# Softmax sums, folds and statistics placed differently in a planned attention kernel: all sums on VectorE, and a planner that keeps GpSimd and VectorE's two-operand sums apart

## The chip, the cores and the metric

The kernel runs on one core of a Trainium2 chip. The metric is the device time of one execution in microseconds (us), and the median over several executions counts. The engines of the core run side by side, each through its own queue of instructions in order: TensorE (PE in the profile, with PEld for its weight loads), VectorE (DVE), ScalarE (ACT), GpSimd (POOL) and SyncE (SP), which here issues nearly all DMAs. They meet through semaphores.

## The reference

A cross attention is followed by a small recurrent state space layer, all in float32:

```
xn   = layernorm(x)          # x: 4096 x 512
cn   = layernorm(ctx)        # ctx: 3202 x 512
x    = x + softmax(q(xn) k(cn)^T / 8) v(cn) W_o + b_o      # 8 heads of 64
U    = (layernorm(x) W_in + b_in) B                        # 4096 x 64
s_t  = silu(s_{t-1} A^T) + u_t                             # over the 4096 rows
out  = x + s C + mean(program_probs) W_prog + b_prog
```

## The kernel before

**Tiles and stages.** A first stage (to about 200 us) normalizes the context and writes keys and values to DRAM (`kd`, `vd`). Then comes the attention. The queries are cut into 8 blocks Q of 512 rows, the heads into 4 pairs `hp`, and each pair works on two halves of 256 queries. One such (Q, hp, half) is a *unit*; there are 64. A unit goes over the 3202 keys in `NDC` = 13 steps c of 256 keys (the last step is half as wide; two left-over keys are handled apart, as the "extra" tile). In each step:

- `scores` (PE, L635): eight matmuls on quarters of the array into one PSUM tile `s`. There are two such tiles (ring `s`).
- `weights` (ACT, L705): the exponential of the tile, PSUM to SBUF tile `p`, 128x1024. There are 18 such tiles (ring `p`).
- `product` (PE, L745): weights times values into the output accumulator `po` in PSUM. There is one such accumulator (ring `o`), so the first product of a unit waits until the last unit's has been emptied.
- `add` (L713): the weights are added elementwise into `acc`, 128x1024, to be the softmax's denominators. It is a tensor_tensor with both operands in SBUF. Step 1 adds the tiles of step 0 and 1, the others add to `acc`. Of the steps c = 2, 6 and 10 the add runs on GpSimd (`POOL_SUMS`), except in the last unit; all others run on VectorE.

After step 1, `rest` (VectorE, L699) adds the two left-over keys in two small instructions.

**The end of a unit** (`finish`): `output` (ACT, L780) copies one half of `po`, and `join` (VectorE, L784) adds the other half from PSUM, which frees `po`. `fold` (GpSimd, L720) adds the two halves of `acc`, `sums` (PE, L763, tile `pd`) adds over the partitions, two copies on ScalarE (L797) and `whole` (VectorE, L801) collect the denominators, `inverse` (VectorE, L804) takes the reciprocal, `scale` (VectorE, L811) multiplies the output by it, and `fall` (L807) sums it for a check.

**Beside the units.** For each block of queries: `queries` (layer norm, transposition and the query projection of the next block; `heads`, L312) and `project` (output projection `outs` L988, residual `x1` L1001, a second layer norm, the inputs `u` of the recurrence, L1044). Both use `norm_pieces`: `stats` (VectorE), `factors` (three small GpSimd instructions), `scaled` (ACT). GpSimd also adds two rows of constants, `row` (L982) and `mod` (L1005). Two halves of 128 rows belong together; each half's `stats` takes one of two places in the ring `fs`.

**The end of the kernel** (`drain`). The recurrence is computed by sweeps over 16 steps that repeat until start and end agree; sweep "a" runs beside the last units, sweep "b" and a chain for the last 256 rows (`last_rows`, L1420) after them. Each link of a chain goes PE (L1179), ACT (L1207, L1417), VectorE (L1214, L1420). `outputs` joins the states' products (L1253) with the rows (VectorE L1273; ACT L1267 and GpSimd L1270), and DMAs store them. Last comes a check: `differ` compares the sweeps, `nbad` (L1799) is read by all engines, and a branch skips a slow repair.

**What sets the order.** The order of all this is planned when the program is built. `Plan.add` records a piece: engine, an assumed cost in ns, the pieces that it follows, a due time, and the ring places that it takes and gives. `Plan.order` plays the pieces through: whenever an engine is free it takes, of those that are ready and find their ring places (`fits`), the one with the earliest due time. A piece on another engine can start `LATE` ns after the end of the one that it follows; `ENTER` and `LEAVE` are added where TensorE changes between quarter matmuls (`kind` "quarters") and full ones. Only the order comes of it. On the chip, each engine goes through its queue in that order and waits on semaphores. `from_(d)` ties a piece to the scores of the step at due time d, and `STEP` = 2150 ns is one step in due times.

Of the kernel before, what the change touches and what calls it, by code (L numbers as in the profile page):

```python
# [10 lines left out]
F32 = mybir.dt.float32  # L11
# [3 lines left out]
ALU = mybir.AluOpType  # L15
# [5 lines left out]
P = 128  # L21
# [4 lines left out]
NDC = NCH // 2  # L26
# [12 lines left out]
NP = 18  # L39
# [9 lines left out]
STEP = 2150  # L49
# [18 lines left out]
class Plan:  # L68
# [31 lines left out]
    def order(self):  # L100
# [10 lines left out]
        free = dict.fromkeys(self.LATE, 0)  # L111
        last, now, events, out = None, 0, [], []
# [58 lines left out]
def xattn_ssm_kernel(  # L171
# [534 lines left out]

    def add(w, c, engine):
# [5 lines left out]
        engine.tensor_tensor(  # L713
            w["acc"][:, :, :nb, :], t[:, :, :nb, :], before[:, :, :nb, :], ALU.add
        )

    def fold(w):

        acc = w["acc"]
        nc.gpsimd.tensor_tensor(acc[:, :, 0, :], acc[:, :, 0, :], acc[:, :, 1, :], ALU.add)  # L720

# [64 lines left out]
    def finish(w, i, d, plan):  # L786
# [22 lines left out]
        def scale(part):  # L809
# [28 lines left out]
    def norm_pieces(plan, ks, gets, d, after, names, gives, wait):  # L838
# [21 lines left out]
        for t, (k, v) in enumerate(zip(ks, vs)):  # L860
            plan.add((*k, "stats"), "DVE", 870, partial(stats_, v, gets[t], names[t]), [after[t]],
                     d + t, ["fs"])
            plan.add((*k, "factors"), "POOL", 2000, partial(factors_, v), [(*k, "stats")], d + 2000)
            plan.add((*k, "scaled"), "ACT", 800, partial(scaled_, v, gets[t], t),
                     [(*k, "factors")] + ([(*ks[0], "scaled")] if t else []) + wait, d + 3 * STEP + t,
                     [] if t else ["xh", "xh"], [("fs", (*k, "stats"))] + gives[t : t + 1])
        return vs
# [98 lines left out]
    def project(plan, Q, halves, d, index):  # L966

        for half in halves:
# [42 lines left out]
            for t in range(2):  # L1011
                plan.add((*ks[t], "load"), "SP", 800, partial(load, t),
                         [(*ks[0], "load")] if t else [from_(d - 6 * STEP)], d - 6 * STEP + t, [] if t else ["x"])
                plan.add((*ks[t], "row"), "POOL", 1300, partial(row, vs[t]), [(*ks[t], "load")], d - STEP)
            plan.add((*k2, "outs"), "PE", 7200, outs,
# [101 lines left out]
    AHEAD_K, AHEAD, REF = 10, 6, 5  # L1117
    POOL_SUMS = (2, 6, 10)
    A_PACE, B_PACE = 1500, 1900
# [359 lines left out]
    def unit(plan, i):  # L1479
# [30 lines left out]
        for c in range(NDC):  # L1510
# [17 lines left out]
            if c:  # L1528
                dve = w["last"] or c not in POOL_SUMS
                before = {1: ("weights", i, 0), 2: ("rest", i)}.get(c, ("add", i, c - 1))  # L1530
                plan.add(("add", i, c), "DVE" if dve else "POOL", (100 + 1200 * part) if dve else 2382,
                         partial(add, w, c, nc.vector if dve else nc.gpsimd),
                         [("weights", i, c), before], d + 1200,
                         ["acc"] if c == 1 else [],
                         [p] + ([("p", ("weights", i, 0))] if c == 1 else []))
            if c == 1:
                plan.add(("rest", i), "DVE", 1200, partial(rest, w), [("add", i, 1), ("extra", first)],
                         d + 1300, [], [("extra", ("extra", first))])
# [228 lines left out]
    with tc.manual_schedule():  # L1767
        for g in range(AHEAD_K):
            load_k(*steps[g])
        for g in range(AHEAD):  # L1770
            load_v(*steps[g])
        plan = Plan(
            dict(
                s=2, m=2, mt=1, o=1, p=NP, acc=3, extra=4, q=6, x=2, x1=1, xn2=1, fs=2,
                xn=1, xh=2, max=2, rd=2, o_=12,
# [113 lines left out]
```

## Time and profile before

| what | value |
|---|---|
| median of 3 runs | 2004.89 us (2004.11 to 2006.86) |
| the profiled execution's own time | 2004.45 us |
| its span | 2002.6 us |
| mean granted clock of TensorE | 0.995 |
| busy: PE, DVE, ACT, POOL | 1954.1, 1259.4, 1130.1, 789.5 us |
| scores (L635) and products (L745), 12800 matmuls each | 826.5 and 822.6 us |
| adds (L713) on VectorE, on GpSimd | 515 + 64, 189 |
| HBM | 93 GB/s over the span |

The profile shows one execution. "Busy" is time with an instruction of that engine in work; matmuls overlap and their ends are modelled, so a short wait of TensorE can be hidden behind the end of the matmul before, and the distance from one start to the next tells more. In a row of groups stand line, engine, operation, tiles and shapes, the number of instructions, busy us and mean ns of one, then the idle time of the engine in front of them and what ended it. In a row in order of time stand start, length, engine, line, operation, tiles, shapes, number, and in brackets the idle time in front.

### The profile page before, as it was taken

What the parts mean: (1) busy time and instruction counts of PE and PEld (TensorE: products, weight loads), DVE (VectorE), ACT (ScalarE), POOL (GpSimd) and SP (SyncE); (2) the same over time, 40 slices, a digit from 0 to 9 for tenths busy, and PEclk for the clock granted to TensorE, in tenths of its full rate; (3) what the DMA queues carried; (4) which work ended last, traced back from release to release, by engine and by line L of the source; (5) the groups of instructions that cost most, each with busy time, mean ns of one, the idle gap of its engine ahead of it and who ended that gap; (6) DMA issues with size and microseconds to landing.
All of it is one profiled execution on the core that took longest, in us unless ns stands there. A gap on an engine that the chain in (4) does not pass through costs nothing. (4 is left out here: it accounts for less than half of the span.)

```text
span 2002.6 us, 66617 instructions
## 1 busy us (share of the span) xinstructions
PE 1954.1 (98%) x29070; PEld 1251.4 (62%) x29070; DVE 1259.4 (63%) x1533; ACT 1130.1 (56%) x1478; POOL 789.5 (39%) x631
## 2 busy tenths in 40 slices
PE   8999999999999999999999999999999999999996
PEld 4444566666666666666666666666666666666764
DVE  4311367566866677667756785667766675667575
ACT  2233466566666566556656665666565666655552
POOL 2111234345533454245434543445334642444424
PEclk9999999999999999999999999999999999999998
DMA  5632323224332243123322332234322331444485
GB/s 173 192 100 66 101 80 97 58 79 111 106 79 79 82 112 92 59 81 90 107 65 79 106 107 73 79 95 113 86 78 59 101 92 52 148 142 144 129 207 182
DMA packets 246934, 204.28 MB, mean 102 GB/s; under 512 B 80808, under 2 KB 220072, under 8 KB 246636
## 3 DMA queue, kind: packets, MB, share of 16 engines
q1 hardware_dynamic: 242088, 192.28, 33.4%
q10 hardware_dynamic: 4548, 7.67, 1.2%
q8 instruction: 231, 3.78, 0.8%
q14 instruction: 67, 0.55, 0.1%
HBM read 156.32 MB, written 29.88 MB: 93 GB/s over the span
## 5 line engine op out<-in xcount | busy, mean ns | idle before, releaser
L705 ACT ACTIVATE p<-s,shifts 128x1024 f32<-128x1024 f32 (+1 forms) x832 | 883.2, 1080 | 559.7 <-PE s L635 540.0
L745 PE MATMUL po<-p,v 64*64 64x256 f32 x12800 | 822.6, 377 | 10.6 <-DVE o L784 10.6
L635 PE MATMUL s<-q,k 64*64 64x256 f32 x12800 | 826.5, 377 | 4.9 <-ACT p L705 3.9
L713 DVE TENSOR_TENSOR acc<-p,acc 128x1024 f32<-128x1024 f32 (+1 forms) x515 | 633.3, 1230 | 249.0 <-POOL acc L713 179.4
L713 POOL TENSOR_TENSOR acc<-p,acc 128x1024 f32<-128x1024 f32 x189 | 449.2, 2376 | 679.1 <-ACT p L705 362.2
L635 PEld LDWEIGHTS s<-q,k 64*64 64x64 f32 x12800 | 482.6, 133 | 233.3 <-ACT p L705 32.5
L745 PEld LDWEIGHTS po<-p,v 64*64 64x64 f32 x12800 | 487.8, 133 | 209.7 <-DVE o L784 15.2
L720 POOL TENSOR_TENSOR acc<-acc 128x512 f32<-128x512 f32 x64 | 91.5, 1430 | 160.9 <-DVE acc L713 153.3
L713 DVE TENSOR_TENSOR acc<-p,p 128x1024 f32<-128x1024 f32 x64 | 99.5, 1555 | 75.8 <-ACT p L705 70.2
L312 PE MATMUL pq<-xn,wq 128*128 128x512 f32 x256 | 118.3, 605 | 0.0
L804 DVE RECIPROCAL rd<-rd 128x256 f32<-128x256 f32 (+1 forms) x65 | 112.4, 1729 | 2.2
L988 PE MATMUL pa<-wo,o 128*128 128x512 f32 x240 | 107.0, 599 | 0.0
L699 DVE TENSOR_TENSOR acc<-x,acc 2x256 f32<-2x256 f32 x128 | 95.2, 744 | 2.5
L551 PE MATMUL pv<-wv,ct 128*128 128x512 f32 (+1 forms) x208 | 95.5, 611 | 1.0 <-ACT ct L519 0.7
L584 PE MATMUL pk<-ct,wk 128*128 128x512 f32 (+1 forms) x224 | 88.8, 549 | 0.0
L312 PEld LDWEIGHTS pq<-xn,wq 128*128 128x128 f32 x256 | 46.0, 189 | 57.6 <-issue 57.5
L784 DVE TENSOR_TENSOR o<-po,o 128x256 f32<-128x256 f32 x64 | 27.1, 423 | 84.3 <-ACT o L780 83.7
L988 PEld LDWEIGHTS pa<-wo,o 128*128 128x128 f32 x240 | 44.4, 190 | 56.0 <-issue 53.7
L321 ACT ACTIVATE q<-pq,bias 128x512 f32<-128x512 f32 x32 | 22.0, 687 | 98.4 <-PE pq L312 98.4
L519 DVE COPY ct<-tp_c 128x512 f32<-128x512 f32 (+1 forms) x13 | 8.5, 651 | 104.1 <-PE tp_c L283 104.1
L584 PEld LDWEIGHTS pk<-ct,wk 128*128 128x128 f32 x224 | 39.2, 190 | 42.6 <-issue 42.6
L551 PEld LDWEIGHTS pv<-wv,ct 128*128 128x128 f32 (+1 forms) x208 | 38.1, 192 | 44.3 <-issue 42.1
(215 smaller groups left out, 1200.3 us busy)
## 6 DMA issues: line engine op xcount, KB each, us to landing
k<-kd SPq DMA_DIRECT2D x432, 128.0 KB, 2.2
v<-vd SPq DMA_DIRECT2D x432, 128.0 KB, 2.3
xn<-x SPq DMA_DIRECT2D x416, 32.0 KB, 1.9
xr<-in_x_dram SPq DMA_DIRECT2D x30, 256.0 KB, 3.7
x1d<-xr SPq DMA_DIRECT2D x30, 256.0 KB, 3.4
x<-in_x_dram SPq DMA_DIRECT2D x28, 256.0 KB, 3.2
cx<-in_ctx_dram SPq DMA_DIRECT2D x25, 256.0 KB, 2.9
vd<-vs SPq DMA_DIRECT2D x25, 256.0 KB, 2.4
```

The costliest lines, as they stand in the source:

```text
L312: nc.tensor.matmul(pq, wq[:, i, hp * P : (hp + 1) * P], xn[:, i, :], start=(i == 0), stop=(i == NC - 1),)
L551: nc.tensor.matmul(pv[h * HD : h * HD + n, :H], ct[:, k, o : o + n], wv[:, k, :], start=(i == 0), stop=(i == NC // parts - 1), skip_group_ ...
L584: nc.tensor.matmul(pk[:, :n_g], wk[:, i, hp * P : (hp + 1) * P], ct[:, i, :n_g], start=(i == 0), stop=(i == NC - 1),)
L635: nc.tensor.matmul(s[k0 : k0 + HD, a, b, :], kts[(*w["at"][:2], c)][r, b * CK + k0 : b * CK + k0 + HD], q[r], start=True, stop=True, skip_ ...
L699: nc.vector.tensor_tensor(to[r], t[r], to[r], ALU.add)
L705: nc.scalar.activation(t[:, :, :nb, :], w["ps"][c][:, :, :nb, :], AF.Exp, bias=w["shift"])
L713: engine.tensor_tensor(w["acc"][:, :, :nb, :], t[:, :, :nb, :], before[:, :, :nb, :], ALU.add)
L720: nc.gpsimd.tensor_tensor(acc[:, :, 0, :], acc[:, :, 0, :], acc[:, :, 1, :], ALU.add)
L745: nc.tensor.matmul(w["po"][a * HD : (a + 1) * HD, k, :QU], vts[Q, hp, c][r, b, a * HD : (a + 1) * HD], t[r, a, b, :], start=(c == 0 and b ...
L784: nc.vector.tensor_tensor(o, rows_of(w, w["po"][:, 1, :QU], True), o, ALU.add)
L804: nc.vector.reciprocal(w["rd"][:, part], w["rd"][:, part])
L988: nc.tensor.matmul(v["pa"], o_t[Q, c, half][:, t * P : (t + 1) * P], wo[:, c, :], start=(c == 0), stop=(c == NC - 1),)
```

## The change

Six things change together.

1. All adds run on VectorE; `POOL_SUMS` is gone. Their assumed cost is 120 + 1120 ns instead of 100 + 1200 (or 2382 on GpSimd).
2. `fold` runs on VectorE, with an assumed cost of 680 ns.
3. `sums` may come from 2 steps after the unit's end on, where it was 6.
4. The planner no longer lets a GpSimd piece and a VectorE piece named add, rest, fold or scale run at the same time (`PORT`, `shares`).
5. From VectorE to another engine the planner assumes 500 ns, where it was 130.
6. In `norm_pieces`, the first half's statistics take two places of the ring `fs` (now 4) for both halves, and the second half's follow the first's; small tiles have four buffers. The assumed cost of `row` is 1270 ns, that of `rest` 860.

The number of matmuls and of adds stays the same, and what is computed too.

```diff
-    LATE = {"PE": 110, "DVE": 130, "ACT": 110, "POOL": 100, "SP": 5000}
+    LATE = {"PE": 110, "DVE": 500, "ACT": 110, "POOL": 100, "SP": 5000}
...
+    PORT = ("add", "rest", "fold", "scale")
...
+        def shares(p):
+            return p["engine"] == "POOL" or p["engine"] == "DVE" and p["name"][0] in self.PORT

         def fits(p):
+            if port > now and shares(p):
+                return False
...
                 free[e] = now + cost
+                if shares(p):
+                    port = free[e]
...
-        engine.tensor_tensor(
+        nc.vector.tensor_tensor(
             w["acc"][:, :, :nb, :], t[:, :, :nb, :], before[:, :, :nb, :], ALU.add
...
-        nc.gpsimd.tensor_tensor(acc[:, :, 0, :], acc[:, :, 0, :], acc[:, :, 1, :], ALU.add)
+        nc.vector.tensor_tensor(acc[:, :, 0, :], acc[:, :, 0, :], acc[:, :, 1, :], ALU.add)
...
-        plan.add(("fold", i), "POOL", 1620, partial(fold, w), [("add", i, NDC - 1)], d + 500)
+        plan.add(("fold", i), "DVE", 680, partial(fold, w), [("add", i, NDC - 1)], d + 500)
...
-                 [("fold", i)] + ([] if last else [from_(d + 6 * STEP)]), d + 1000,
+                 [("fold", i)] + ([] if last else [from_(d + 2 * STEP)]), d + 1000,
...
-                v[k] = ln.tile([P, n], F32, tag=f"{k}_2", name=f"{k}_{name}")
+                v[k] = ln.tile([P, n], F32, tag=f"{k}_2", name=f"{k}_{name}", bufs=4)
...
-            plan.add((*k, "stats"), "DVE", 870, partial(stats_, v, gets[t], names[t]), [after[t]],
-                     d + t, ["fs"])
+            plan.add((*k, "stats"), "DVE", 870, partial(stats_, v, gets[t], names[t]),
+                     [after[t]] + ([(*ks[0], "stats")] if t else []),
+                     d + t, [] if t else ["fs", "fs"])
...
-                dve = w["last"] or c not in POOL_SUMS
...
-                plan.add(("add", i, c), "DVE" if dve else "POOL", (100 + 1200 * part) if dve else 2382,
-                         partial(add, w, c, nc.vector if dve else nc.gpsimd),
+                plan.add(("add", i, c), "DVE", 120 + 1120 * part, partial(add, w, c),
```

More of the change, by code (lines that the diff above doesn't have):

```diff
@@ L111, in order @@
         free = dict.fromkeys(self.LATE, 0)
-        last, now, events, out = None, 0, [], []
+        last, now, port, events, out = None, 0, 0, [], []
+        def shares(p):
+            return p["engine"] == "POOL" or p["engine"] == "DVE" and p["name"][0] in self.PORT
         def fits(p):
+            if port > now and shares(p):
+                return False
             for r in set(p["take"]):
@@ L705, in weights, with add @@
         nc.scalar.activation(t[:, :, :nb, :], w["ps"][c][:, :, :nb, :], AF.Exp, bias=w["shift"])
-    def add(w, c, engine):
+    def add(w, c):
         nb, t = blocks(c), w["s"][c]
@@ L865, in norm_pieces @@
                      [(*k, "factors")] + ([(*ks[0], "scaled")] if t else []) + wait, d + 3 * STEP + t,
-                     [] if t else ["xh", "xh"], [("fs", (*k, "stats"))] + gives[t : t + 1])
+                     [] if t else ["xh", "xh"], [("fs", (*ks[0], "stats"))] + gives[t : t + 1])
         return vs
@@ L1013, in project @@
                          [(*ks[0], "load")] if t else [from_(d - 6 * STEP)], d - 6 * STEP + t, [] if t else ["x"])
-                plan.add((*ks[t], "row"), "POOL", 1300, partial(row, vs[t]), [(*ks[t], "load")], d - STEP)
+                plan.add((*ks[t], "row"), "POOL", 1270, partial(row, vs[t]), [(*ks[t], "load")], d - STEP)
             plan.add((*k2, "outs"), "PE", 7200, outs,
@@ L1536, in unit @@
             if c == 1:
-                plan.add(("rest", i), "DVE", 1200, partial(rest, w), [("add", i, 1), ("extra", first)],
+                plan.add(("rest", i), "DVE", 860, partial(rest, w), [("add", i, 1), ("extra", first)],
                          d + 1300, [], [("extra", ("extra", first))])
@@ L1773, in xattn_ssm_kernel @@
             dict(
-                s=2, m=2, mt=1, o=1, p=NP, acc=3, extra=4, q=6, x=2, x1=1, xn2=1, fs=2,
+                s=2, m=2, mt=1, o=1, p=NP, acc=3, extra=4, q=6, x=2, x1=1, xn2=1, fs=4,
                 xn=1, xh=2, max=2, rd=2, o_=12,
```

1 line of the change is left out of this document (removed).

## The prediction

> **What bounds the kernel now.** I read the engines' busy times first, then the stretches, then what TensorE waits for.
>
> ```profile
> PE 1954.1 (98%) x29070; PEld 1251.4 (62%) x29070; DVE 1259.4 (63%) x1533; ACT 1130.1 (56%) x1478; POOL 789.5 (39%) x631
> ```
>
> ```profile
> 200.00:1937.30 1737.30, 1720.02 (x28016) 1134.34 (x28014) 1167.29 (x1307) 1050.59 (x1327) 726.34 (x490) 1.00 0.34 95
> 1937.30:2002.60 65.30, 43.39 (x494) 25.27 (x490) 37.25 (x104) 18.00 (x56) 29.09 (x38) 0.89 0.65 198
> ```
>
> ```profile
> PE po L745 <- DVE o L784: 10.6, 8, 2.6
> PE s L635 <- ACT p L705: 3.9, 10, 0.4
> PE pu L1044 <- DMA xn<-x: 1.1, 1, 1.1
> ```
>
> The second fence is the busy time by stretch: length, then PE, PEld, DVE, ACT, POOL. TensorE bounds the kernel. In the attention stretch (200 to 1937.3 us) it is idle for 17.3 us of 1737.3, and the third fence (TensorE's waits: total, times, longest) names 15.6 of them. The edit takes no work from TensorE: the matmuls are the same, and counted in the two programs' orders the changes between quarter-array and full-array matmuls are as many (366 and 364 runs). So neither the shorter adds nor an empty GpSimd is a gain by itself. Only TensorE's waits, and the last 65.3 us, which is a serial chain, can move.
>
> **The largest wait.** VectorE and GpSimd hold each other up; first the groups by shape, with two rows of one tile's instructions (min/median/max ns):
>
> ```profile
> L713 DVE TENSOR_TENSOR acc<-p,acc 128x1024 f32<-128x1024 f32 x451 | 585.3, 1298 | 243.9 <-POOL acc L713 179.4 <-ACT p L705 44.7 <-DVE acc L713 0.5
> L713 DVE TENSOR_TENSOR acc<-p,acc 128x512 f32<-128x512 f32 x64 | 48.4, 756 | 5.2
> L713 POOL TENSOR_TENSOR acc<-p,acc 128x1024 f32<-128x1024 f32 x189 | 449.2, 2376 | 679.1 <-ACT p L705 362.2 <-DVE acc L713 248.6 <-DVE acc L699 53.5
> L720 POOL TENSOR_TENSOR acc<-acc 128x512 f32<-128x512 f32 x64 | 91.5, 1430 | 160.9 <-DVE acc L713 153.3 <-DMA xr<-in_x_dram 4.3 <-DMA v<-vd 3.3
> L982 POOL TENSOR_TENSOR xr<-xr,rowb 128x512 f32<-128x512 f32 x30 | 52.8, 1772 | 19.8 <-DMA xr<-in_x_dram 14.5 <-issue 5.3
> ...
> L713 DVE TENSOR_TENSOR acc<-p,acc x515: 686/1225/3228, 231.9 to 1937.1; 128x1024 f32<-128x1024 f32 x151, 128x512 f32<-128x512 f32 x21
> L699 DVE TENSOR_TENSOR acc<-x,acc x128: 404/416/2618, 228.4 to 1920.5; 2x256 f32<-2x256 f32 x128
> ```
>
> Then one place in order of time:
>
> ```profile
> 538.87 2.92 DVE L699 TENSOR_TENSOR acc<-x,acc 2x256 f32<-2x256 f32 x2
> 538.93 2.58 POOL L713 TENSOR_TENSOR acc<-p,acc 128x1024 f32<-128x1024 f32 x1
> 539.31 2.00 PE L635 MATMUL s<-q,k 64*64 64x256 f32 x32
> 540.06 0.37 ACT L780 COPY o<-po 128x256 f32<-128x256 f32 x1
> 541.82 0.42 DVE L784 TENSOR_TENSOR o<-po,o 128x256 f32<-128x256 f32 x1
> 541.93 2.37 POOL L713 TENSOR_TENSOR acc<-p,acc 128x1024 f32<-128x1024 f32 x1 [0.43 <-DVE acc L699]
> 542.16 3.23 DVE L713 TENSOR_TENSOR acc<-p,acc 128x1024 f32<-128x1024 f32 x1
> 542.30 1.53 PE L745 MATMUL po<-p,v 64*64 64x256 f32 x24 [0.99 <-DVE o L784]
> ```
>
> An add that VectorE does in 1.225 us took 3.23 beside a GpSimd add; the join (L784), which reads one operand from PSUM, keeps its 0.42. Two small adds (L699, 0.42 each) took 2.92 together, and the join stood behind them. The next unit's first product needs the join, because the output accumulator has one buffer. The Trainium skill ("SBUF — State Buffer", section "Who interferes with whom") calls this an exclusive lock: a VectorE instruction with two SBUF inputs and a GpSimd instruction that reads SBUF exclude each other for a whole instruction. The rows agree.
>
> **The change, part by part.**
>
> *Work moved.* 189 adds of 1.225 us are 232 us more on VectorE; 64 folds cost, by the 128x512 add, 0.69 to 0.76 each, 44 to 48 us. GpSimd loses 449.2 + 91.5 and keeps 249. Contention that goes returns (1.298 - 1.225) x 451 = 33 us on the chained adds if none is left. VectorE ends at 1500 to 1540 us, 75 to 77%. It stays under TensorE, so this counts nothing while no join, fold or maximum comes late (second rival).
>
> *Join waits.* All eight have a GpSimd add on the port in front of the join, and no such add is left. Two scores pieces normally take 1.73 us (249.24 to 250.97 below); here the product came 2.99 after, so 1.26 was lost where 0.99 shows: 0.27 more for each. Gone: 10.6 + 8 x 0.27 = 12.8 us; lower bound 10.6 less a few that stay, say 8.
>
> *Clock.* The longest of the eight was followed by this stretch (same columns; the third number from the end is the granted clock):
>
> ```profile
> 328.90:332.30 3.40, 3.40 (x40) 2.15 (x36) 3.30 (x4) 0.00 (x0) 0.13 (x1) 0.51 0.02 5
> ```
>
> 3.4 us at 0.51 cost 1.7 us, which go with the wait. The Trainium skill ("TensorE: Matmul & The Clock Gate", section "HAM oscillation — how this bites in real kernels") warns of idle gaps above about 3.4 us; by that the wait of under 3 us would have cost no clock and the sum would be 1.7 us less gain. Here a shorter one did it, and the row decides.
>
> *The planner's order.* It now takes 500 ns instead of 130 from VectorE to another engine, so it puts more TensorE work between the last product of a unit and the first of the next. Counted in the two orders: before, 40 of 63 boundaries have just two scores pieces there; after, 44 have scores, scores, sums, scores and 9 have scores, scores, sums. The join gets 0.86 x 3 + 0.43 = 3.0 us where 1.73 has been enough (first two rows below). But scores have two PSUM buffers, and a third piece must wait for ScalarE to empty the first:
>
> ```profile
> 249.24 1.91 PE L635 MATMUL s<-q,k 64*64 64x256 f32 x32
> 250.97 1.26 PE L745 MATMUL po<-p,v 64*64 64x256 f32 x20
> ...
> 483.33 1.92 PE L635 MATMUL s<-q,k 64*64 64x256 f32 x32
> 485.67 1.09 PE L635 MATMUL s<-q,k 64*64 64x256 f32 x16 [0.42 <-ACT p L705]
> 486.58 0.61 PE L745 MATMUL po<-p,v 64*64 64x256 f32 x8
> ...
> 574.74 1.04 PE L635 MATMUL s<-q,k 64*64 64x256 f32 x16
> 575.61 0.61 PE L653 MATMUL sm<-q,kx 64*64 64x256 f32 x8
> 576.04 1.04 PE L745 MATMUL po<-p,v 64*64 64x256 f32 x16
> 577.07 1.09 PE L635 MATMUL s<-q,k 64*64 64x256 f32 x16
> 577.99 0.39 PE L763 MATMUL pd<-acc,ones 64*64 64x256 f32 x3
> ```
>
> A buffer is free 2.33 to 2.34 us after its scores began (574.74 to 577.07; 483.33 to 485.67). Three scores in a row want it after 1.73: 0.61 lost, and the piece behind the wait takes 0.91 instead of 0.86. Scores, scores, sums, scores wants it after 0.86 + 0.86 + 0.43 = 2.16, as in the rows from 574.74: 0.17 lost and again 0.06. So 44 x 0.23 = 10.1 us are new; between nothing (the copy happens to be early) and 44 x 0.66 = 29 (as if the sums gave no time), I take the row with the same 2.16. Three in a row are 16 instead of 9: 7 x 0.66 = 4.6. The pattern from 574.74 itself occurs 17 instead of 23 times: 6 x 0.23 = 1.4 back. The one DMA wait of 1.1 us goes too: its matmuls now stand after later scores.
>
> *Attention in sum:* 12.8 + 1.7 + 1.1 + 1.4 - 10.1 - 4.6 = 2.3 us gained.
>
> *Statistics in pairs, row cost, rest cost.* No instruction is added; they only move places in the order. VectorE's queue and the planned 2-microsecond factors on GpSimd cover them: nothing. If a flip came late, the SyncE moves behind it would hold later K and V loads, which are issued 10 and 6 steps ahead.
>
> *The end.* Rows of TensorE, then of VectorE:
>
> ```profile
> 1937.41 3.70 PE L1335 MATMUL yb<-wo,o 128*128 128x512 f32 x8
> 1941.04 0.66 PE L763 MATMUL pd_last<-acc,ones 64*64 64x256 f32 x8
> 1944.57 2.31 PE L1335 MATMUL yb<-wo,o 128*128 128x512 f32 x4 [0.96 <-DVE o L811]
> ...
> 1978.35 0.29 DVE L1214 SCALAR_TENSOR_TENSOR scan<-scan,z 128x128 f32<-128x128 f32 x1 [0.15 <-ACT scan L1207]
> 1986.44 0.29 DVE L1429 TENSOR_TENSOR scan<-scan 128x128 f32<-128x128 f32 x1
> 1990.51 0.68 DVE L1467 SCALAR_TENSOR_TENSOR xr_l<-py_o,xr_l 128x512 f32<-128x512 f32 x1
> 1994.65 0.69 DVE L1273 SCALAR_TENSOR_TENSOR row<-py,row 128x512 f32<-128x512 f32 x1 [1.67 <-ACT y_l L1267]
> 1995.26 0.14 DVE L1799 CAST nbad<-pbad 1x1 int32<-1x1 f32 x1
> ```
>
> The last sums now stand behind four projection matmuls instead of eight, so the wait of 0.96 goes: 1.0 us. At the very end the flag (L1799) stood behind four output rows (L1273), 1995.26 against 1990.51 + 0.68 = 1991.19; in the new order all these rows come before the second scan ends, so 4.1 us go. Three of them now lie between the first scan's end and the second's (1978.35 to 1986.44): 3 x 0.68 less what a link's TensorE and ScalarE time hides, I take 1.2 back, between 0 and 2. How the first scan's sixteen steps share VectorE with more rows is open, 2 us either way, taken as nothing. Gained: 3.9.
>
> *Sum:* 2.3 + 3.9 = 6.2 us. The profiled execution took 2004.45 us (span 2002.6), 0.44 under the median of 2004.89. 2004.89 - 6.2 = 1998.7; I say 1998.5.
>
> **Rivals.**
> - *No change.* The scans share VectorE badly and the end gains nothing, while attention gains its 2.3: 2002.6; with ten more waits of 0.61 it is 2008.7. For it: four of six terms are small differences of counts. Against: the flag's place at the end is fixed by the order.
> - *VectorE late: slower.* Each join and fold stands behind adds that a remaining GpSimd add can hold (30 of 1.77 us at L982, as many in the order at L1005). If a third of the 60 fall near a boundary and each delays the join by half of 1.77 beyond its slack, that is 18 us, less the 6.2 above: 2017; with a fifth, 2009. It decides from a mean lateness of 0.1 us on each of 63 boundaries (6.2 / 63). Against: the join has some 1.3 us more slack than before. The lock rule of the Trainium skill, named above, stands behind this: all 253 instructions moved to VectorE become exposed to what GpSimd keeps.
> - *The ring costs nothing.* If the third scores never wait, 10 us more are gained: 1988.5. The rows from 574.74 speak against it.
>
> **How the numbers follow.** Forecast 0.56 (own range 1994 to 2001), no change 0.24, VectorE late 0.13, ring free 0.07. A measurement here tells 0.2%, 4 us, from no change: under 2000.9 is faster. Forecast and free ring give 0.63, then 0.24 and 0.13. The range leaves out about 0.07 below and 0.1 above: 1992 to 2008.
>
> **What would show it.** TensorE's waits: the join's 10.6 near nothing, the wait for ScalarE (L635) above 3.9 with many more times, idle short since 0.17 hides behind modelled ends: so I look at starts, 2.33 from the first to the third scores. L713 (acc<-p,acc) on VectorE x704, the full shape at a mean near 1.23; POOL near 249 busy; no stretch under full clock between 200 and 1930. At the end the flag comes within 0.3 us of L1467. Wrong would be: waits for L720 or L784 that add up to more than 6 us, or a last L1214 more than 43 us after the first yb (here 40.9).

## The result, and the profile after

The changed kernel takes **1998.7 us** (median of 7 runs, 1998.34 to 2000.9), the kernel before 2005.46 us (median of 7, 2004.11 to 2006.86) beside it: a ratio of 0.9969, 95% interval 0.9958 to 0.9981. It is faster by 6.8 us, and the interval leaves out 1. The prediction said 1998.5. The profiled execution took 2000.26 us (span 1998.4), so it lies 1.56 above the median, and 4.2 us of span are what its trace has to explain.

The code between the prediction's lines moved by 8: scores are L643, products L753, weights L713, adds L721, rest L707, fold L728, the join L792, sums L771; at the end z is L1187, the chains L1222 and L1428, rows L1281, the last output L1475, the flag L1805.

The busy times, the stretches (length, PE, PEld, DVE, ACT, POOL, granted clock, DMA share, GB/s) and TensorE's waits (total, times, longest):

```profile
PE 1959.9 (98%) x29070; PEld 1250.2 (63%) x29070; DVE 1442.1 (72%) x1786; ACT 1126.5 (56%) x1478; POOL 235.3 (12%) x378
```

```profile
200.00:1934.10 1734.10, 1723.73 (x28016) 1131.45 (x28014) 1349.92 (x1558) 1047.87 (x1327) 175.92 (x240) 1.00 0.34 95
1934.10:1998.40 64.30, 45.35 (x492) 26.98 (x490) 37.48 (x106) 17.11 (x56) 25.32 (x35) 0.84 0.63 197
```

```profile
PE s L643 <- ACT p L713: 7.5, 17, 0.7
PE pu L1053 <- DMA xn<-x: 1.2, 1, 1.2
PE pd_last L771 <- DVE acc L728: 0.3, 1, 0.3
```

The waits for the join, 10.6 us in eight places, are gone; the wait for ScalarE, that is for a score buffer, has grown from 3.9 in 10 to 7.5 in 17. Attention ends 3.3 us earlier (the first yb starts at 1934.14, before at 1937.41), the end is 0.9 shorter (64.24 for 65.19). The adds have lost most of their contention, 1.245 for 1.298 us (VectorE's adds, number, busy us and mean ns first):

```profile
L721 DVE TENSOR_TENSOR acc<-p,acc 128x1024 f32<-128x1024 f32 x640 | 797.0, 1245 | 178.2 <-ACT p L713 145.6 <-DVE acc L721 0.5
```

TensorE in order of time shows both kinds of ring wait, that is of waits for one of the two score buffers; the rows from 479.25 are three scores in a row, those from 560.78 the sums between scores:

```profile
479.25 1.92 PE L643 MATMUL s<-q,k 64*64 64x256 f32 x32
481.59 1.09 PE L643 MATMUL s<-q,k 64*64 64x256 f32 x16 [0.42 <-ACT p L713]
...
560.78 0.61 PE L771 MATMUL pd<-acc,ones 64*64 64x256 f32 x8
561.34 1.09 PE L643 MATMUL s<-q,k 64*64 64x256 f32 x16
562.25 2.77 PE L753 MATMUL po<-p,v 64*64 64x256 f32 x48
```

The third scores start 2.34 after the first: 0.61 lost, and 0.05 in the piece behind (481.59 to 482.50), as predicted. Behind the sums, 560.78 to 562.25 are 1.47 us where sums and scores need 0.43 + 0.87: 0.17 lost, less than the predicted 0.23. That is the median of the 44 places. The prediction's rows from 574.74 were not typical of their pattern: there the third scores began 2.33 us after the first, but in the median of the 23 places of the kernel before 2.28, which is 0.17 lost as well.

The end, TensorE first:

```profile
1934.14 1.98 PE L1343 MATMUL yb<-wo,o 128*128 128x512 f32 x4
1936.42 0.66 PE L771 MATMUL pd_last<-acc,ones 64*64 64x256 f32 x8 [0.29 <-DVE acc L728]
1937.01 5.42 PE L1343 MATMUL yb<-wo,o 128*128 128x512 f32 x12
1942.36 0.43 PE L1187 MATMUL z<-scan,a_t 64*64 64x128 f32 x4
```

```profile
1952.90 0.29 DVE L1222 SCALAR_TENSOR_TENSOR scan<-scan,z 128x128 f32<-128x128 f32 x1 [3.54 <-ACT scan L1215]
...
1979.15 0.29 DVE L1222 SCALAR_TENSOR_TENSOR scan<-scan,z 128x128 f32<-128x128 f32 x1
...
1987.83 0.29 DVE L1437 TENSOR_TENSOR scan<-scan 128x128 f32<-128x128 f32 x1
...
1990.97 0.68 DVE L1475 SCALAR_TENSOR_TENSOR xr_l<-py_o,xr_l 128x512 f32<-128x512 f32 x1
1991.57 0.14 DVE L1805 CAST nbad<-pbad 1x1 int32<-1x1 f32 x1
```

From the first yb to the first z it is 8.2 us (before 9.4). The flag comes straight behind L1475: from the second scan's end to the flag 3.7 us, before 8.8. But the first scan, from z to the last L1222, takes 36.8 us, before 31.5 (1946.82 to 1978.35).

### The profile page after: what moved, and what is told of

Its sections match the earlier page's. It is cut to its first block, busy times and chain, and to the rows that moved or that the text cites. A ratio compares the mean times of both kernels' runs of the same rounds, so it can differ in the third digit from the quotient of the medians.

```text
span 1998.4 us, 66546 instructions
## 1 busy us (share of the span) xinstructions
PE 1959.9 (98%) x29070; PEld 1250.2 (63%) x29070; DVE 1442.1 (72%) x1786; ACT 1126.5 (56%) x1478; POOL 235.3 (12%) x378
## 4 chain that ended last, share of the span: by engine, by line
PE 95%; DVE 2%; ACT 1%; issue 1%; DMA 1%; SPq 0%; POOL 0%; ACTq 0%; DVEq 0%; POOLq 0%
PE s L643 35%; PE po L753 34%; PE pq L320 6%; PE pa L997 5%; PE pk L592 4%; PE pv L559 4%; PE pd L771 1%; ACT p L713 1%; PE pu L1053 1%; PE sm L661 1%; PE po L741 1%; PE tp_c L291 0%; PE za L1187 0%; DVE row L1281 0%; PE sm L680 0%
## 5 line engine op out<-in xcount | busy, mean ns | idle before, releaser
L713 ACT ACTIVATE p<-s,shifts 128x1024 f32<-128x1024 f32 (+1 forms) x832 | 885.4, 1080 | 552.2 <-PE s L643 543.4
L721 DVE TENSOR_TENSOR acc<-p,acc 128x1024 f32<-128x1024 f32 (+1 forms) x704 | 842.3, 1196 | 185.5 <-ACT p L713 146.0
L643 PE MATMUL s<-q,k 64*64 64x256 f32 x12800 | 831.4, 378 | 8.6 <-ACT p L713 7.5
L753 PE MATMUL po<-p,v 64*64 64x256 f32 x12800 | 813.3, 376 | 0.0
L643 PEld LDWEIGHTS s<-q,k 64*64 64x64 f32 x12800 | 477.8, 133 | 251.2 <-ACT p L713 54.8
L753 PEld LDWEIGHTS po<-p,v 64*64 64x64 f32 x12800 | 491.1, 133 | 187.8 <-issue 2.4
L991 POOL TENSOR_TENSOR xr<-xr,rowb 128x512 f32<-128x512 f32 x30 | 55.2, 1857 | 892.3 <-DMA xr<-in_x_dram 467.5
L721 DVE TENSOR_TENSOR acc<-p,p 128x1024 f32<-128x1024 f32 x64 | 82.5, 1288 | 69.6 <-ACT p L713 64.0
L1014 POOL TENSOR_TENSOR xr<-x,modb 128x512 f32<-128x512 f32 x30 | 38.1, 1271 | 427.7 <-DVE x L1010 427.7
L707 DVE TENSOR_TENSOR acc<-x,acc 2x256 f32<-2x256 f32 x128 | 61.4, 480 | 2.9
L600 ACT ACTIVATE ks<-pk,bias 128x512 f32<-128x512 f32 (+1 forms) x28 | 18.0, 642 | 75.4 <-PE pk L592 68.3
```

What stands on the lines that cost most here:

```text
L643: nc.tensor.matmul(s[k0 : k0 + HD, a, b, :], kts[(*w["at"][:2], c)][r, b * CK + k0 : b * CK + k0 + HD], q[r], start=True, stop=True, skip_ ...
L707: nc.vector.tensor_tensor(to[r], t[r], to[r], ALU.add)
L713: nc.scalar.activation(t[:, :, :nb, :], w["ps"][c][:, :, :nb, :], AF.Exp, bias=w["shift"])
L721: nc.vector.tensor_tensor(w["acc"][:, :, :nb, :], t[:, :, :nb, :], before[:, :, :nb, :], ALU.add)
L753: nc.tensor.matmul(w["po"][a * HD : (a + 1) * HD, k, :QU], vts[Q, hp, c][r, b, a * HD : (a + 1) * HD], t[r, a, b, :], start=(c == 0 and b ...
L991: nc.gpsimd.tensor_tensor(v["x"], v["x"], rowb, ALU.add)
```

## The experiments

Each run was compared with the kernel before in the same set; ratios are to it, with 95% intervals. "Attention" is from the first scores' start to the first yb's in the trace, "end" from there to the end of the span; the waits are TensorE's for the join and for ScalarE at the scores, in us (times). Ratios come from several executions, the other columns from one: the changed kernel's two traces (changed, e9) differ by 1.3 us in the end alone.

| run | ratio | attention | end | join | scores |
|---|---|---|---|---|---|
| before | 1 | 1721.2 | 65.2 | 10.6 (8) | 3.9 (10) |
| changed | 0.9969 (0.9958 to 0.9981) | 1717.8 | 64.2 | none | 7.5 (17) |
| changed, again (e9) | 0.9966 (0.9954 to 0.9978) | 1717.5 | 62.9 | none | 7.5 (17) |
| e1 end planned with 130 | 0.9991 (0.9981 to 1.0) | 1720.7 | 64.7 | 1.9 (1) | 7.2 (16) |
| e2 attention planned with 130 | 0.9943 (0.993 to 0.9957) | 1715.9 | 63.7 | 1.1 (1) | 2.8 (8) |
| e3 before, adds moved | 1.001 (1.0001 to 1.0019) | 1721.8 | 68.1 | 14.3 (17) | 0.3 (1) |
| e4 before, 500 ns | 0.9983 (0.9974 to 0.9992) | 1720.2 | 62.6 | 3.4 (2) | 5.7 (18) |
| e5 no exclusion | 0.9973 (0.9962 to 0.9984) | 1719.1 | 61.4 | none | 6.5 (16) |
| e6 fold back | 0.9976 (0.9966 to 0.9985) | 1720.5 | 65.3 | none | 9.3 (24) |
| e7 e2 and late sums | 1.0055 (1.0041 to 1.0068) | 1727.1 | 72.4 | 12.9 (13) | 4.0 (11) |
| e8 adds back | 1.0006 (0.9997 to 1.0015) | 1724.0 | 63.9 | 1.7 (3) | 9.6 (19) |
| e10 attention planned with 350 | 0.9932 (0.9918 to 0.9946) | 1709.6 | 63.3 | none | 2.9 (7) |
| e11 before, adds, folds, early sums | 0.9947 (0.9934 to 0.9961) | 1707.6 | 67.7 | none | 0.4 (1) |
| e12 e10 without exclusion | 0.9974 (0.9963 to 0.9984) | 1716.8 | 64.5 | 3.9 (5) | 0.4 (1) |

**The 500 ns, split between end and attention (e1, e2).** A piece's place in the plan tells whether `drain` added it:

```diff
-                heapq.heappush(events, (free[e] + self.LATE[e], 1, p["at"], p))
+                heapq.heappush(events, (free[e] + (130 if e == "DVE" and p["at"] >= self.tail else 500 if e == "DVE" else self.LATE[e]), 1, p["at"], p))
...
-        drain(plan)
+        plan.tail = len(plan.pieces); drain(plan)
```

> The changed kernel, but for the pieces of the end (drain) the planner takes 130 ns again from VectorE to another engine; the attention's order keeps its pattern (44 boundaries with scores, scores, sums, scores; 15 threes in a row for 16). Theory (the 500 ns alone set the end's order, both its gain and its loss): the first scan, from its first z to its last L1222, falls from 36.8 to 31.5 +-1 us, four rows L1281 stand between L1475 and the flag again, and L.states to the flag goes from 3.7 to 8 to 9 us; together 1998.7 - 5.3 - 0.6 + 5.1 = 1998, within 2 us. Rival (the first scan is slow for another reason, as the clock, which was half for 6.8 us there): it stays above 35 us, the flag's loss comes alone, and the time is 2002 to 2004.

Measured: 2005.2 us (2001.73 to 2007.12, 11 runs), beyond both expectations. The end's order did what the theory said: the first scan took 32.9 us, and the flag came 9.2 us after the second scan, behind four rows again:

```profile
1989.49 0.68 DVE L1475 SCALAR_TENSOR_TENSOR xr_l<-py_o,xr_l 128x512 f32<-128x512 f32 x1
1990.09 0.68 DVE L1281 SCALAR_TENSOR_TENSOR row<-py,row 128x512 f32<-128x512 f32 x1
...
1993.59 0.69 DVE L1281 SCALAR_TENSOR_TENSOR row<-py,row 128x512 f32<-128x512 f32 x1 [1.62 <-ACT y_l L1275]
1994.20 0.14 DVE L1805 CAST nbad<-pbad 1x1 int32<-1x1 f32 x1
```

What neither theory had is that the end's pieces also order the last units. Counted from the first scores, both traces agree within 0.1 us up to the 57th join; 3.0 us are lost at the units behind it, most of it here, where a reciprocal stands in front of a join:

```profile
1915.50 1.75 DVE L812 RECIPROCAL rd<-rd 128x256 f32<-128x256 f32 x1
...
1918.40 0.41 DVE L792 TENSOR_TENSOR o<-po,o 128x256 f32<-128x256 f32 x1
```

```profile
1918.86 2.44 PE L753 MATMUL po<-p,v 64*64 64x256 f32 x24 [1.93 <-DVE o L792]
```

After this wait TensorE ran at half clock for 3.4 us from 1919.3, which is 1.7 of the 3.0 us.

So the 500 ns are worth 0.0022 to 0.0025 of the time (about 4.5 us) by what they do to the end and the last units.

e2 is the same edit the other way round (500 for the pieces of `drain`, 130 for the others).

> The changed kernel, but for the attention the planner takes 130 ns again, and 500 for the pieces of the end, whose order stays the same. In the order: scores, scores, sums, scores 37 times for 44, three scores in a row 7 for 16. Theory (the waits for the score buffers are priced as the prediction has them, 0.23 and 0.66 each, and the join needs no more room than two scores): 7 x 0.23 + 9 x 0.66 = 7.6 us faster, 1991 to 1993; TensorE's wait for the join (L792) stays under 2 us. Rival (the 500 ns protect the joins): the join waits come back, 0.1 to 0.2 us on each of 63 boundaries, and the time is 1997 to 2004.

Measured: 1996.71 us, 0.9943; against the changed kernel's 0.9969 some 5 us less. The price of three scores in a row holds: the wait for ScalarE falls by 4.7 us; reckoned from the matmuls' starts it is 7 (9 times three scores in a row fewer, at 0.66, and 7 of the other pattern, at 0.17). But its joins and folds came late where they had not before (below: wait of the sums for the fold, of the inputs for a DMA, of the product for the join), which takes most of it back in the trace. The room that 500 ns give was worth something, and cost more.

```profile
PE s L643 <- ACT p L713: 2.8, 8, 0.4
PE pd L771 <- DVE acc L728: 1.8, 5, 0.5
PE pu L1053 <- DMA xn<-x: 1.3, 2, 1.1
PE po L753 <- DVE o L792: 1.1, 1, 1.1
```

And 37 of the 44 boundaries with the sums between scores are still there, with 130 ns: these do not come from the 500.

**The adds alone (e3), the 500 ns alone (e4).**

```diff
-    POOL_SUMS = (2, 6, 10)
+    POOL_SUMS = ()
```

> The kernel before, with all adds on VectorE and nothing else changed: no 500 ns, no exclusion, folds on GpSimd, sums six steps later, statistics one by one. In the order: three scores in a row once (9 before, 16 after), scores, scores, sums, scores never, scores, sample, product, scores 31 times (23 before). Theory (the adds on GpSimd were what held the joins; the ring waits are all placed by the planner): 14.5 for the joins and the clock, 8 x 0.66 for the threes, less 8 x 0.23, so 2005.5 - 14.5 - 5.3 + 1.8 = 1987.5, 1985 to 1990. Rival A (the folds that stay on GpSimd, 64 of 1.43 us, now hold the adds and joins): waits for the join of 4 to 8 us stay, 1992 to 1997. Rival B (the planner's parts bring the gain): 2003 to 2006.

Measured: 2008.09 us, 1.001: nothing gained. The prediction's account of the join waits falls here: not one add is left on GpSimd, and TensorE waits more for the join than before.

```profile
PE po L745 <- DVE o L784: 14.3, 17, 1.5
PE yb L1335 <- DVE o L811: 2.9, 1, 2.9
```

One of the longest, on VectorE, on GpSimd and on TensorE:

```profile
641.35 2.20 DVE L713 TENSOR_TENSOR acc<-p,p 128x1024 f32<-128x1024 f32 x1 [1.56 <-ACT p L705]
643.58 1.83 DVE L699 TENSOR_TENSOR acc<-x,acc 2x256 f32<-2x256 f32 x2
645.52 1.23 DVE L713 TENSOR_TENSOR acc<-p,acc 128x1024 f32<-128x1024 f32 x1
646.66 0.42 DVE L784 TENSOR_TENSOR o<-po,o 128x256 f32<-128x256 f32 x1
```

```profile
641.18 1.28 POOL L982 TENSOR_TENSOR xr<-xr,rowb 128x512 f32<-128x512 f32 x1
643.84 1.29 POOL L982 TENSOR_TENSOR xr<-xr,rowb 128x512 f32<-128x512 f32 x1 [1.38 <-DMA xr<-in_x_dram]
```

```profile
647.14 1.96 PE L745 MATMUL po<-p,v 64*64 64x256 f32 x32 [1.38 <-DVE o L784]
```

Two rows on GpSimd, which stayed there, take VectorE's add from 1.23 to 2.20 us and its two small adds from 0.84 to 1.83; a further add stands in front of the join that GpSimd used to do. At other places a fold does the same: eight of the 17 late joins follow a row (10.4 us of waits), nine a fold (3.9). What GpSimd held up is enough for all 17: at each, the adds, rests and folds of the last 7 us took 0.96 to 2.11 us longer than unhindered, and the product then waited 0.31 to 1.52. The 2.9 of the second line is the last scaling, late for the output projection: the end is 68.1 us long.

```diff
-    LATE = {"PE": 110, "DVE": 130, "ACT": 110, "POOL": 100, "SP": 5000}
+    LATE = {"PE": 110, "DVE": 500, "ACT": 110, "POOL": 100, "SP": 5000}
```

> The kernel before with 500 ns for 130 alone; adds and folds on GpSimd as before. In the order: three scores in a row 26 times for 9 (7 of them behind a sample or a projection), scores, sample, product, scores 31 for 23; the end's order is that of the changed kernel. Theory: 17 x 0.66 + 8 x 0.23 = 13 us lost on the score buffers; the joins have 0.86 more room at these boundaries, so that half to all of the 12.8 go, and the end gives 0 to 3: 2003 to 2010, taken as 2006. Rival (the lateness alone brings the change's gain): 1998 to 2000.

Measured: 2003.21 us, 0.9983, inside the theory's range and lower than its 2006. With all 189 adds on GpSimd, room alone brings the join from 10.6 to 3.4 us, and the ring takes it back; the gain is at the end, 62.6 us. The traced execution is the fastest of the 11 (2000.73 us), so its end may flatter the run.

**Exclusion, fold, sums, adds, each undone in the changed kernel (e5 to e8).** After e3 the theory was revised: whatever runs on GpSimd beside a sum in front of the join delays it, and the planner must keep them apart or leave room.

```diff
-            if port > now and shares(p):
+            if False:
```

> The changed kernel, but the planner lets GpSimd and VectorE's two-operand sums run at the same time again; adds and folds stay on VectorE, the 500 ns stay. In the order: scores, scores, sums, scores 53 times for 44, three scores in a row 15 for 16. Revised theory (any GpSimd instruction beside an add or a rest in front of the join makes it late, so the exclusion is needed, but the 500 ns leave room): the ring costs 9 x 0.13 - 0.6 = 0.6 more; of waits like the seven of 1.55 us in the run with the adds alone, 0.3 to 1.5 each stay: 2 to 10 us slower than the changed kernel, so 0.998 to 1.002 of the kernel before. Rival (with adds and folds on VectorE there is nothing left that matters on GpSimd): within 1 us of the changed kernel, 0.9965 to 0.9975.

Measured: 1999.87 us, 0.9973: with 500 ns of room, the exclusion shows nothing, as the rival had it. The attention is 1.3 us longer, the end 2.8 shorter, without the half clock in the first scan that the changed kernel's trace has. Nor does the exclusion keep the engines apart on the chip: the 640 adds take 1.245 us on average with it and without, a small add of rest 0.480 and 0.483.

```diff
-        nc.vector.tensor_tensor(acc[:, :, 0, :], acc[:, :, 0, :], acc[:, :, 1, :], ALU.add)
+        nc.gpsimd.tensor_tensor(acc[:, :, 0, :], acc[:, :, 0, :], acc[:, :, 1, :], ALU.add)
...
-        plan.add(("fold", i), "DVE", 680, partial(fold, w), [("add", i, NDC - 1)], d + 500)
+        plan.add(("fold", i), "POOL", 1620, partial(fold, w), [("add", i, NDC - 1)], d + 500)
```

> The changed kernel with the 64 folds on GpSimd again (cost 1620 in the plan), the exclusion and the 500 ns kept. In the order: three scores in a row 23 for 16, scores, scores, sums, scores 28 for 44. By the measured prices (0.6 for a three, 0.13 for the other): 7 x 0.6 - 16 x 0.13 = 2.1 us slower. Revised theory (kept apart by the plan, a fold on GpSimd harms nothing): 0.998 +-0.001 of the kernel before, waits for the join under 2 us. Rival (folds must be on VectorE): waits for join or fold of over 4 us, at or above the kernel before.

Measured: 2001.63 us, 0.9976, no wait for a join: as the theory had it, 1 to 2 us above the changed kernel, which the intervals don't separate.

e7 is e2 with one more edit:

```diff
-                 [("fold", i)] + ([] if last else [from_(d + 2 * STEP)]), d + 1000,
+                 [("fold", i)] + ([] if last else [from_(d + 6 * STEP)]), d + 1000,
```

> The changed kernel with 130 ns for the attention, 500 for the end, and the sums from 6 steps after the unit's end again. In the order: scores, scores, sums, scores never, three scores in a row 10 times. Theory: against the run with 130 ns for the attention, the waits for the ring behind the sums (4.1) and of the sums for the fold (1.8 to 2.8) go, 3 threes come: 4 to 6 us less than that run's 0.9943, so 0.9915 to 0.993. Rival (the sums between the scores are what gives the join its room): waits for the join (L792) of 5 us and more come back as in the run with the adds alone, 0.995 to 1.0.

Measured: 2017.92 us, 1.0055. This is 0.0112 of the time, some 22 us, slower than e2, and both expectations miss it; the waits for the join are of the rival's kind, at 12.9 us. In the traces the attention is 11.2 us longer and the end 8.7: the last sums wait 2.4, the last scaling 2.9, and half clock covers 17 us of the projection and the first scan, for 6.8 in e2. One of the join waits, VectorE, ScalarE and TensorE:

```profile
722.20 0.69 DVE L728 TENSOR_TENSOR acc<-acc 128x512 f32<-128x512 f32 x1
722.81 1.22 DVE L721 TENSOR_TENSOR acc<-p,p 128x1024 f32<-128x1024 f32 x1
724.06 0.84 DVE L707 TENSOR_TENSOR acc<-x,acc 2x256 f32<-2x256 f32 x2
724.93 0.42 DVE L792 TENSOR_TENSOR o<-po,o 128x256 f32<-128x256 f32 x1
```

```profile
722.40 0.36 ACT L788 COPY o<-po 128x256 f32<-128x256 f32 x1
```

```profile
725.41 1.96 PE L753 MATMUL po<-p,v 64*64 64x256 f32 x32 [1.72 <-DVE o L792]
```

Nothing on GpSimd is in the way here. The join could start at 722.76, and stands 2.17 us behind a fold, the next unit's first add and its rest, all VectorE's own. Six of the 13 late joins are of this kind (7.4 us); ahead of the other seven (5.5 us) rows on GpSimd held VectorE's sums up, as in e3. Two things come with early sums, and no run separates them. The first is VectorE's queue: with sums at 2 steps the reciprocal (1.75 us) follows the join by 3.3 us (median), with 6 steps by 14.4. Taking from each VectorE instruction the part that falls into the 10 us ahead of a join, and the mean over the 62 inner joins, VectorE is busy for 8.5 of the 10 us in this run and 8.2 in e3, against 7.1 in e2 and 7.2 in e11, where the sums are early; the join comes over 1 us behind the copy at 21 and 28 boundaries, against 8 and 3. The second is the expectation's rival, the room: the early sums stand between the scores at 37 boundaries in e2 and 33 in e11, never here or in e3. At each of these 70 the join ended less than 1.47 us ahead of the first product, and 1.47 us is what sums and third scores take there; behind two scores alone, the product would have waited for a join as late as that.

e8 gives the adds back to GpSimd:

```diff
+    POOL_SUMS = (2, 6, 10); A_PACE, B_PACE = 1500, 1900
...
-                plan.add(("add", i, c), "DVE", 120 + 1120 * part, partial(add, w, c),
+                dve = w["last"] or c not in POOL_SUMS
+                plan.add(("add", i, c), "DVE" if dve else "POOL", (120 + 1120 * part) if dve else 2382,
+                         partial(add, w, c, nc.vector if dve else nc.gpsimd),
```

> The changed kernel with the adds of steps 2, 6 and 10 on GpSimd again (cost 2382 in the plan), all else as changed: folds on VectorE, exclusion, 500 ns, pairs. In the order: three scores in a row 21 for 16, scores, scores, sums, scores 6 for 44. Revised theory (what matters is that the planner keeps them apart, not on which engine the adds run): 5 x 0.6 - 38 x 0.13 = 2 us less by the ring, joins quiet; 0.996 to 0.998. Rival (the adds had to leave GpSimd, as the prediction had it): waits for the join of 5 to 11 us, 0.999 to 1.003.

Measured: 2006.94 us, 1.0006. The adds do have to leave GpSimd, by 7.5 us, but not for the rival's reason: the joins wait only 1.7. The attention is 6.2 us longer, and the named waits have grown by 7.2: a score buffer 2.6 us late at one place (9.6 in all for 7.5), DMAs of the inputs 4.6 in 3 places for 1.2, the join 1.7. The trace shows what made the buffer late (GpSimd, ScalarE, TensorE):

```profile
1856.32 2.37 POOL L721 TENSOR_TENSOR acc<-p,acc 128x1024 f32<-128x1024 f32 x1 [4.06 <-DVE acc L721]
...
1860.02 1.07 POOL L858 TENSOR_SCALAR rstd_y<-mv_y 128x1 f32<-128x1 f32 x1
```

```profile
1862.70 0.81 ACT L866 ACTIVATE xh_y<-x,nm_y,rstd_y 128x512 f32<-128x512 f32 x1 [3.82 <-POOL nm_y L860]
```

```profile
1864.57 1.09 PE L643 MATMUL s<-q,k 64*64 64x256 f32 x16 [2.60 <-ACT p L713]
```

The statistics were done at 1857.72, but the small `factors` stood behind an add and a `mod` on GpSimd and ended 4.94 us later (1.80 in the median); `scaled` waited for them on ScalarE, and the next exponential behind `scaled`. After the wait TensorE ran at half clock for 3.4 us, 1.7 us more. What made the DMAs late stays open.

**What the gain consists of (e9 to e12).** e9 is the changed kernel beside the others.

> The changed kernel itself, beside the others of this set, as their measure: 0.9969 of the kernel before as at first, 0.996 to 0.998.

Measured: 1998.68 us, 0.9966.

e11 takes the kernel before, and only moves the adds and folds and lets the sums come early (the edits shown for e3, and those of e6 and e7 the other way round):

> The kernel before with three parts of the change: adds and folds on VectorE, and the sums from 2 steps after the unit's end; 130 ns, no exclusion, statistics one by one. In the order: three scores in a row once, scores, scores, sums, scores 33 times, scores, sample, product, scores 17. Theory (with everything on VectorE it is the early sums that keep its work away from the join: with sums 6 steps later joins waited 13 to 14 us in two runs): waits for the join under 5 us for 14.3 with the adds alone; 33 x 0.13 = 4.3 more for the ring; the end without the 2.9 of the late scaling: 0.994 to 0.9975. Rival (the lateness or the exclusion hold the joins): waits for the join of 10 us and more, at or above 0.999.

Measured: 1994.29 us, 0.9947, as the theory had it. It is faster than the whole change, and its attention is the shortest of all, 13.6 us under the kernel before (the stretch to its end, columns as above):

```profile
200.00:1924.40 1724.40, 1719.86 (x28017) 1132.60 (x28015) 1348.17 (x1556) 1049.19 (x1327) 189.49 (x240) 1.00 0.34 96
```

No product waits for a join, without exclusion and with 130 ns, and 33 boundaries with the sums between scores stand in its order. Against e3 only moved folds and early sums were added, for 14.2 us of attention; its end is as slow as e3's, by the late scaling (2.8) and the flag.

e10 keeps the changed kernel and takes 350 in the place of e2's 130:

> The changed kernel with 350 ns instead of 500 for the attention, 500 for the end. In the order: three scores in a row 7 times and scores, scores, sums, scores 37, as with 130 (16 and 44 with 500). Theory (the ring waits fall as with 130, and the room that 350 gives keeps joins and folds from coming late): the 2.9 us that joins and folds cost with 130 go as well, 0.992 to 0.9935. Rival (what the attention gains does not hang on this number between 130 and 500): 0.9943 to 0.997.

Measured: **1991.5 us** (1990.97 to 1993.39, 5 runs), 0.9932, as the theory had it, and faster than both kernels: 14.2 us under the kernel before and 7.2 under the changed one in the same set. The interval reaches e2's 0.9943, so 350 against 130 is not settled by the times; against 500 it is. Its order has as few threes (three scores in a row) as e2's, and the waits for join and fold are gone, but for 0.6 of the last sums:

```profile
PE s L643 <- ACT p L713: 2.9, 7, 0.4
...
PE pd_last L771 <- DVE acc L728: 0.6, 1, 0.6
```

The attention is 6.3 us shorter than e2's, more than the 2.9 of the theory; what the rest is stays open.

e12 is e10 with e5's edit as well.

> As the run with 350 ns, and without the exclusion. In the order: three scores in a row once, scores, scores, sums, scores 53 times; ring waits 53 x 0.13 + 0.6 = 7.5 against 37 x 0.13 + 7 x 0.6 = 9.0. Theory (the exclusion was worth nothing beside 500 ns): within 2 us of the run with 350 ns, 0.992 to 0.994. Rival (the exclusion matters once the room is less): joins and folds late by 3 to 8 us, 0.995 to 0.998.

Measured: 2000.6 us, 0.9974: the rival's number. Joins wait 3.9, DMAs of the inputs 3.3, and the last scaling is late (2.9). But its order differs from e10's in more than the neighbours of GpSimd, and in e11 no product waited for a join without exclusion, so this run doesn't show that the exclusion is what is missing.

## Why the prediction was right, and where it was not

The time, 1998.5 against 1998.7, and the sign came out; some of the terms did not, and the cause given for the largest was only half of it. That it came to 0.2 us is luck: in the two traces the attention gave 1.1 us more than forecast and the end 3.0 less, and the span differs by 4.2, not 6.2.

- **Join waits, 12.8: gone, as predicted; the reason was incomplete.** The step read "All eight have a GpSimd add on the port in front of the join, and no such add is left." It holds for seven of them; ahead of the join at 1586.43 us it was a fold, of 2.19 us. e3 took exactly these adds away, and 14.3 us of join waits stood in their place, behind sums that rows and folds on GpSimd held up; in e7 more than half of the waits stood behind VectorE's own work alone. That is the rival "VectorE late", which the change escapes by its early sums (e7 against e2; e11 against e3, with the folds), not by having moved the adds alone.
- **Clock, 1.7: right.** The attention stays at full clock (1.00 in its stretch). **The DMA wait of 1.1: wrong**, 1.2 us remain.
- **The ring: price nearly right, origin half wrong.** 0.66 for three scores in a row holds, and they come from the 500 ns: 16 with 500, 7 with 130 or 350. The other pattern cost 0.17 for 0.23, so 44 x 0.17 = 7.5 for 10.1 (the prediction priced it by one untypical place), and "It now takes 500 ns ... so it puts more TensorE work" was not its cause: it stays with 130 (37 of them) and stands 33 times in e11; it comes with the sums two steps after the unit.
- **Attention: 3.4 us gained for 2.3.** With the measured sizes, 12.8 + 1.7 - 0.1 + 6 x 0.17 - 7.5 - 4.6, the sum is 3.3. The small net is the difference of two large terms: e11's attention gains 13.6, and the changed kernel keeps 3.4 of it.
- **VectorE's busy time: 1442 us, not 1500 to 1540.** The prediction gave back contention for the chained adds alone, 33 us. The small adds of rest fell from 95.2 to 61.4 us too, the first adds of the units from 99.5 to 82.5 and the scalings from 37.8 to 26.6, 62 us in all. VectorE stays under TensorE, so the time doesn't show it.
- **The end: the sums' wait 1.2 for 1.0, the flag 5.1 for 4.1, both by the mechanism named.** The rows between the scans took 0.6 back for 1.2 (8.7 us from scan to scan for 8.1). The flag's 5.1 has 0.9 in it that was not foreseen (last section).
- **The failed step: "How the first scan's sixteen steps share VectorE with more rows is open, 2 us either way, taken as nothing."** It cost 5.3 us, and the last L1222 came 45.0 us after the first yb, past the prediction's own sign of 43. Half of it is the order: in e4 and e5, which have the changed kernel's order of the end and full clock there, the scan takes 34.1 and 34.3, 2.5 to 2.7 over before. The other 2.5 to 2.7 is a stretch at half clock that the prediction had not expected at the end. The other traces with this order of the end bear it out, but for e7: the scan takes 34.1 in e12, with no half clock in it, 35.4 to 35.5 in e8, e9 and e10, with 3.4 us of it, and 36.6 to 36.8 in the changed kernel, e2 and e6, with 6.8; in e7, whose first links come late, 37.5. So the end gave 0.9 for 3.9 in this execution, and 2.2 in e9's (62.9).
- **Against the rivals.** "No change" and "VectorE late" came out in other members of the same family: e1 and e8 have the time of the first, though not its mechanism, and e3 and e7 show the second at work. In the changed kernel itself the scan did share VectorE badly, as "no change" has it, but the flag made up for it. "The ring costs nothing" gave 1988.5; e10, with fewer ring waits, measured 1991.5.
- **Statistics in pairs** and the other costs in the plan were never undone alone; "nothing" for them stays untested.

## What to carry to other kernels

When instructions are moved to an engine that is only three quarters busy, look at what then stands in its queue ahead of the one instruction that the bottleneck waits for, and at what the bottleneck can do meanwhile: moving the adds alone gained nothing, and letting the sums come 4 steps earlier, which changes both, was worth 22 us between two otherwise equal plans, 11 of them in the attention. A planner's lateness is a price with two sides: in the changed kernel's plan 130 ns left joins and folds late by 2.9 us, 500 used up the score buffers, and 350 was 7 us better than 500. No such number holds for every plan: with 130, no product waits for a join in e11. Try it separately for stages with different limits: 500 was better than 130 for the serial end and the last units, and worse than 350 for the rest of the attention.

## What the runs showed of the hardware that was not expected

**Half clock without a pause.** In the changed kernel's end TensorE never paused for even 1 us after 1944.3, yet the clock fell; stretches of the changed kernel, then one of the kernel before (columns as above):

```profile
1944.30:1947.80 3.50, 1.12 (x10) 0.63 (x12) 1.26 (x5) 2.34 (x5) 2.95 (x6) 0.91 0.84 223
1947.80:1954.10 6.30, 6.30 (x32) 4.03 (x31) 0.58 (x2) 1.73 (x4) 1.66 (x3) 0.51 0.24 88
```

```profile
1948.80:1952.80 4.00, 1.85 (x18) 1.20 (x19) 1.14 (x5) 2.51 (x6) 3.52 (x6) 1.00 0.90 239
```

The drop came at 1947.2, inside the first row, and the clock was half for 6.8 us; in the 3.4 us ahead of it TensorE was busy for some 40%. In the third row it was busy for 46% of 4 us without a drop, but these 4 us lie across two steps of 3.4 us with 67 and 57%. Steps of 3.4 us are what the 14 traces show: the half clocks of the attention and the end begin on one grid of 3.4 us in each trace and last 3.4, 6.8 or 10.2 us, except the last of each, which runs into the end of the program. In the 3.4 us ahead of the 33 drops TensorE was busy for 22 to 56%. Every full-clock step of the grid below 45% was followed by a drop, and none above 56%. So the drop goes with the busy share of a step here, not with one long pause: a wait for the join of 1.93 us brought a drop in e1 (43% busy) and none in e7 (49%). One link of the scan in that stretch waited 3.54 us (the row at 1952.90), where it had waited 1.77 before. The Trainium skill ("TensorE: Matmul & The Clock Gate", section "HAM oscillation — how this bites in real kernels") speaks of idle gaps over about 3.4 us; here a thin stream of small matmuls, with gaps under 1 us, did it.

**A one-tile comparison held up by GpSimd.** The comparison with a limit in the check at the end (two instructions, min/median/max ns), in the kernel before and in the changed one:

```profile
L1299 DVE TENSOR_SCALAR scan<-scan x2: 1172/1227/1282, 1980.2 to 1987.7; 128x128 f32<-128x128 f32 x1, 128x32 f32<-128x32 f32 x1
```

```profile
L1307 DVE TENSOR_SCALAR scan<-scan x2: 241/264/288, 1981.2 to 1989.1; 128x128 f32<-128x128 f32 x1, 128x32 f32<-128x32 f32 x1
```

Before, both ran beside GpSimd's row adds of 1.26 us (from 1980.17 and 1987.55) and ended with them. In all runs with the 500 ns at the end it takes 0.26, in those with 130 (e1, e3, e11) 1.23. It has one tensor as input, not two; the Trainium skill ("SBUF — State Buffer", section "Who interferes with whom") names tensor_scalar among those that can take the shared port, which agrees.
